# The tanh of the first layer, chunk by chunk from exponentials and a logarithm

## The chip, the cores and the metric

The kernel runs on one core of a Trainium2 chip. The metric is the device time of one execution in microseconds. The core's engines run side by side, each with its own queue of instructions in program order: TensorE (PE, its weight loads as PEld), VectorE (DVE), ScalarE (ACT), GpSimd (POOL), and SyncE (SP), which issues the transfers.

## The reference, cut to what matters

Eight images of 128 channels by 36 x 36 positions (1296 positions) go through two layers. Layer 0 is a convolutional attention block; the part that the change touches is its last step:

```python
xa = jnp.concatenate([x, a_x], axis=1)
h = jnp.tanh(_conv(xa, w_h, 'VALID') + _bias(b_h))
return _conv(h, w_o, 'VALID') + _bias(b_o)
```

Both convolutions are 1 x 1, so they are matrix products over the channels; the second context's part of the first one is the same for every position and is folded into the bias. Layer 1 is additive attention over the 1296 tokens of an image, followed by a mixture of experts:

```python
t = jnp.tanh(q[:, :, None, :] + k[:, None, :, :])
scores = jnp.einsum('bijd,d->bij', t, w) + bw[0]
attn = jax.nn.softmax(scores, axis=-1)
```

All of it is float32.

## The kernel before, in words

**The main loop.** Nearly all the time goes to the scores of layer 1. The kernel does not form the tanh of every query and key pair. It groups the channels by signs into features, so that a score becomes a sum of fractions: a numerator `n` and a denominator `d`, both products of key features and query features on TensorE (line 963; 968 for the remainder), with `1/d` made on ScalarE as Exp(-Ln(d)) (lines 986 and 989), the product on VectorE (lines 1006 to 1017), and sums on VectorE (`accd`) and GpSimd (`accp`, lines 1024 to 1035). A unit of work is one image, one chunk of 432 queries (three chunks an image) and one tile of 128 keys (ten, and a remainder of 16 keys that takes the sixth place in the order). A unit has 12 slots, the remainder unit two; an image has 366 slots, the whole kernel 2928. In a slot, the denominators of three slots ahead are issued (`LAG = 3`, two PSUM buffers for `d`), then the numerators of this one, then the products. Slots go by threes: the first has a Ln and an Exp for itself, the next two have a Ln each and one Exp of double length. Such a three is called a round below. At the end of a unit the summed scores go through an Exp (line 1046).

**The work beside it.** Everything else is written as generators that stand in four lanes: query features, attention sums, gating of the image before, and `background`. The background lane of image b makes image b + 1 ready: normalisation, the convolutions (`conv_keys`, `layer0`), the layer norm over tokens (`tokens`) and the key features (`keys`). A generator says at each `yield` what it needs next: a turn of matmuls (`matmuls(rest)`), a turn without matmuls (`step(rest)`), or to be taken on at once in the same turn (`TAKE`); `rest` is a number of slots to wait. Matmul turns come in the slots 2, 5, 8 and 11 of a unit, one in each round, and a pace (`PACE`, counted in columns of matmuls) decides how many turns of background a lane gets there. Turns without matmuls come before the denominators of a slot, and the lanes but the first don't get them in the slots 1, 4, 7 and 10 (`take_turns`, line 1086). Whatever is issued this way stands in each engine's queue where the loop put it; there is no other scheduler.

**Around the change.** `layer0(b)` loops over the three chunks of 432 positions. Each begins with the query convolution (`conv_turns`, four turns of three matmuls, whose results VectorE adds up), goes on with its attention (scores, Exp at line 473, `tot` sums on GpSimd at line 464, Ln and Exp of the sum at 487 and 488), and ends with the 1 x 1 convolution, whose result VectorE adds to the attention's part into `hp`, a tile of 128 x 1296 (`hpre` in the profile, line 508). After the third chunk one Tanh over the whole tile, with the bias `hb`, is issued at line 511. [...]there is a table load before it, and line 512 asks for the set with Exp and Ln back directly after it. Two slots later the output convolution (`po`) reads `hp`, and VectorE adds it to the image (line 519). For image 0 all this runs before the main loop, for images 1 to 7 in the background lane.

Of the kernel before, what the change touches and what calls it, by code (L numbers as in the profile page):

```python
# [11 lines left out]
AF = mybir.ActivationFunctionType  # L12
ALU = mybir.AluOpType
AX = mybir.AxisListType

NB, C, H, W = 8, 128, 36, 36
# [6 lines left out]
RC = H // NCH  # L23
# [49 lines left out]
def kernel(  # L73
# [28 lines left out]
    nc = tc.nc  # L102
# [29 lines left out]
    with ExitStack() as loop, ExitStack() as score:  # L132
# [22 lines left out]
        def big_tile(name):  # L155
            return big.tile([128, NT * 128], F32, tag="big", name=name)

        def chunk_tile(name):
            return chunks.tile([128, CH], F32, tag="chunk", name=name)

        def aux(name):
            return ps_n.tile([128, 512], F32, tag="n", name=name)
# [40 lines left out]
        ones = const.tile([128, 128], F32, tag="ones", name="ones")  # L203
# [32 lines left out]
        hb = const.tile([C, 1], F32, tag="hb", name="hb")  # L236
# [20 lines left out]
        LNEXP = "natural_log_exp_and_others"  # L257
# [16 lines left out]
        TAKE = (False, 0)  # L274

        def step(rest=1):
            return (False, rest)

        def matmuls(rest=0):
            return (True, rest)  # L280
# [3 lines left out]
        def bmm(out, lhsT, rhs, **kw):  # L284
            behind[0] += max(out.free_size(), 128) + 20
            mm(out, lhsT, rhs, **kw)  # L286
# [9 lines left out]
        def conv_turns(taps, rows, y0, dst, inner):  # L296

            r0, nr = rows
            even, odd = ((1, slice(1, WV, 2)), (0, slice(0, WV, 2))) if inner else (
                (0, slice(0, W, 2)), (0, slice(1, W, 2)))  # L300
            for j in range(4):
                ps = aux("pc")[:, : nr * HW]
                for dy in range(3):
                    bmm(ps, taps[:, dy, j, :],
                        xwin[:, j, (y0 + dy + r0) * HW : (y0 + dy + r0 + nr) * HW],
                        start=(dy == 0), stop=(dy == 2))
                yield TAKE
                ps = ps.rearrange("p (a b) -> p a b", b=HW)
                for (t0, cols), used in ((even, j < 3), (odd, j > 0)):
                    if used:  # L310
                        d = dst[:, :, cols]
                        m = ps[:, :, t0 : t0 + d.shape[-1]]
                        if j == 0 or (j == 1 and cols is odd[1]):
                            nc.vector.tensor_copy(d, m)
                        elif j == 2 and cols is odd[1]:
                            nc.vector.tensor_sub(d, d, m)
                        else:
                            nc.vector.tensor_add(d, m, d)
                yield matmuls()
# [13 lines left out]
        def load_taps(name):  # L333
            if name in raw_taps:
                return raw_taps.pop(name)[0]
            t = big_tile(name)[:, : 12 * C]
            nc.sync.dma_start(t, turned_taps[name])
            return t.rearrange("p (y j c) -> p y j c", y=3, j=4)
# [68 lines left out]
        def grid(t, width):  # L407
            return t.rearrange("p (a b) -> p a b", b=width)

        def conv_keys(b):  # L410
# [3 lines left out]
            for r0, nr in KROWS:  # L414
                yield from conv_turns(
                    taps["k"], (r0, nr), 1, grid(k[:, r0 * WV : (r0 + nr) * WV], WV), True
                )

        def layer0(b):

            r = xs[b][:, :N]
            k = convolved.pop("k")
            while gates:
                yield step()
            wv_t = load_taps("wv_t")
            v = big_tile("v0")
            wq_t = load_taps("wq_t")
            yield matmuls(3)
            for r0, nr in KROWS:
                yield from conv_turns(  # L430
                    wv_t, (r0, nr), 1, grid(v[:, r0 * WV : (r0 + nr) * WV], WV), True
                )
            yield matmuls(1)

            vw = big_tile("vw")[:DT, : NDT * C].rearrange("p (j c) -> p j c", c=C)
            for g in range(0, NDT, 4):
                some = DTILES[g : g + 4]
                tp = aux("pvw")
                for j, (o, n) in enumerate(some):
                    bmm(tp[:n, j * C : (j + 1) * C], v[:, o : o + n], wh_s[:, 1, :],  # L440
                       start=True, stop=True)
                yield TAKE
                full = sum(n == DT for _, n in some)
                nc.vector.tensor_copy(
                    vw[:, g : g + full, :],
                    tp[:DT, : full * C].rearrange("p (j c) -> p j c", c=C),
                )
                for j in range(full, len(some)):
                    n = some[j][1]
                    nc.vector.tensor_copy(vw[:n, g + j, :], tp[:n, j * C : (j + 1) * C])  # L450
                yield matmuls()
            hp = big_tile("hpre")[:, :N]
            for c in range(NCH):
                cols = slice(c * CH, (c + 1) * CH)
                q = chunk_tile("q0")
                yield from conv_turns(wq_t, (c * RC, RC), 0, grid(q, W), False)
                yield matmuls(1)
                tot = chunk_tile("tot0")
                ex = []

                def total(j):
                    n = DTILES[j][1]
                    of = ex[0] if j == 1 else tot
                    nc.gpsimd.tensor_add(tot[:n], of[:n], ex[j][:n])  # L464

                ax = chunk_tile("ax0")
                for j0 in range(0, NDT + 2, 2):
                    for o, n in DTILES[j0 : j0 + 2]:
                        ps = aux("s0")
                        bmm(ps[:n, :CH], k[:, o : o + n], q, start=True, stop=True)  # L470
                        yield TAKE
                        e = chunk_tile("e0")
                        nc.scalar.activation(e[:n], ps[:n, :CH], AF.Exp)  # L473
                        ex.append(e)
                        if len(ex) > 2:
                            total(len(ex) - 2)
                        yield matmuls()
                    if j0 == 0:
                        continue
                    if j0 == NDT:  # L480
                        total(NDT - 1)
                        yield matmuls(3)
                        ri = chunk_tile("ri0")
                        pt = aux("pt0")
                        bmm(pt[:, :CH], ones[:DT], tot[:DT], start=True, stop=True)
                        yield TAKE
                        nc.scalar.activation(ri, pt[:, :CH], AF.Ln)
                        nc.scalar.activation(ri, ri, AF.Exp, scale=-1.0)
                        yield matmuls()

                    pa = aux("pa0")[:, :CH]
                    for j in (j0 - 2, j0 - 1):
                        n = DTILES[j][1]
                        bmm(pa, vw[:n, j, :], ex[j][:n], start=(j == j0 - 2), stop=(j == j0 - 1))
                    yield TAKE
                    if j0 == 2:
                        nc.vector.tensor_copy(ax, pa)
                    elif j0 < NDT:
                        nc.vector.tensor_add(ax, pa, ax)
                    else:  # L500
                        nc.vector.tensor_add(pa, pa, ax)
                        nc.vector.tensor_mul(ax, pa, ri)
                    yield matmuls()
                px = aux("px1")
                bmm(px[:, :CH].rearrange("p (a b) -> p a b", b=W), wh_s[:, 0, :],
                   xpad[:, 1 + c * RC : 1 + (c + 1) * RC, 1 : 1 + W], start=True, stop=True)
                yield TAKE
                nc.vector.tensor_add(hp[:, cols], px[:, :CH], ax)
                yield matmuls()
            yield step(2)  # L510
            nc.scalar.activation(hp, hp, AF.Tanh, bias=hb)
            nc.scalar.preload_act_table_set(LNEXP)
            yield matmuls(2)
            for c in range(NCH):
                cols = slice(c * CH, (c + 1) * CH)
                po = aux("po0")
                bmm(po[:, :CH], wo_s, hp[:, cols], start=True, stop=True)
                yield TAKE
                nc.vector.scalar_tensor_tensor(
                    r[:, cols], po[:, :CH], bo_s, r[:, cols], ALU.add, ALU.add  # L520
                )
                yield matmuls()
# [611 lines left out]
        for p, (u, k) in enumerate(slots):  # L1134
            b, c, j = units[u]
# [172 lines left out]
    for h in range(NB // 2):  # L1308
        for c in range(NCH):
            cols = slice(c * CH, (c + 1) * CH)  # L1310
# [71 lines left out]
```

## Time and profile before

| what | value |
|---|---|
| median of three runs | 6135.24 us (6124.2 to 6139.08) |
| profiled execution, its own time | 6138.18 us |
| its span, first to last instruction | 6136.4 us |
| mean granted TensorE clock | 0.982 |
| Tanh (line 511), eight of 128 x 1296 | 1.376 us each |
| table loads (lines 511 and 512), eight each | 1.283 us each |
| accp addition on GpSimd (line 1026) | 2.023 us each |

The profile shows one execution. A busy share is an average over the span, and a matmul's end is modelled, so a busy TensorE is not one at its peak. A row of a group gives the line, engine, operation, tiles, shapes and count, then the busy us, the mean ns of one, and how long the engine sat idle before them. In an answer in order of time, the first number is the start in us, the second the length, and a bracket gives the idle time before it and what ended it. The granted clock is the share of full speed that the throttle left to TensorE.

### The profile page before, as it was taken

To read this page: it belongs to the slowest core of one execution; us is meant where nothing else is said; L and a number is where in the kernel's file an instruction comes from. 1 tells how busy PE (TensorE), PEld (TensorE's weight loads), DVE (VectorE), ACT (ScalarE), POOL (GpSimd) and SP (SyncE) were. 2 spreads that over 40 slices of the span, in tenths; PEclk is the share of its full clock that TensorE was granted. 3 is DMA by queue.
4 is the path that set the end of the run, shared out by engine and by line. 5 is a ranking of instruction groups with operands and counts; after the bars stand their busy time and mean duration, and the time that the engine had idled before them with its cause. 6 is when DMAs were issued, how large, how long until landed. Compare 5 with 4: busy or idle time off the path is not lost.

```text
span 6136.4 us, 94187 instructions
## 1 busy us (share of the span) xinstructions
PE 5669.6 (92%) x33480; PEld 2924.0 (48%) x33480; DVE 4787.2 (78%) x9521; ACT 5331.3 (87%) x5851; POOL 4595.9 (75%) x2819
## 2 busy tenths in 40 slices
PE   7999999999999999999999999999999999988886
PEld 5554455544554445544445444454455544534433
DVE  4787878878788788877788777887878878788882
ACT  1999898998989989889998999899998998999990
POOL 4777777787778867778687777877777777777870
PEclk9999999999999999999999999999999999999997
DMA  1200021001110011100111001110011001110008
GB/s 44 73 34 22 25 75 39 20 25 33 67 38 20 26 47 52 37 24 26 59 37 42 22 20 65 40 37 22 25 67 47 21 25 33 57 49 26 28 20 297
DMA packets 151528, 270.95 MB, mean 44 GB/s; under 512 B 45648, under 2 KB 76752, under 8 KB 151056
## 3 DMA queue, kind: packets, MB, share of 16 engines
q1 hardware_dynamic: 151056, 264.92, 13.0%
q8 instruction: 264, 4.33, 0.3%
q14 instruction: 208, 1.70, 0.1%
HBM read 200.41 MB, written 64.19 MB: 43 GB/s over the span
## 4 chain that ended last, share of the span: by engine, by line
PE 54%; DVE 16%; ACT 15%; issue 11%; POOL 2%; DMA 1%; SPq 0%; DVEq 0%; ACTq 0%; POOLq 0%
PE d L963 18%; PE n L963 12%; ACT lq L986 11%; PE pa L286 7%; DVE rp L1017 7%; DVE n L1011 5%; PE pc L286 5%; PE s L286 3%; DVE accd L1013 2%; PE pq L286 2%; PE pk L286 1%; PE d L968 1%; PE n L968 1%; ACT e L1046 1%; DMA w<-in_weight_dram 1%
## 5 line engine op out<-in xcount | busy, mean ns | idle before, releaser
L1026 POOL TENSOR_TENSOR accp<-accp,rp 128x864 f32<-128x864 f32 x1440 | 2912.8, 2023 | 989.4 <-DVE rp L1017 946.2
L963 PE MATMUL d<-qf,kf 32*128 32x432 f32 (+1 forms) x11520 | 2791.6, 563 | 264.8 <-ACT lq L986 259.6
L963 PE MATMUL n<-qf,kf 32*128 32x432 f32 (+1 forms) x11520 | 3001.7, 556 | 28.4 <-DVE rp L1017 10.0
L986 ACT ACTIVATE lq<-d 128x864 f32<-128x864 f32 x2928 | 2481.1, 877 | 471.2 <-PE n L963 288.8
L1017 DVE TENSOR_TENSOR rp<-n,lq 128x432 f32<-128x432 f32 x3912 | 2182.0, 601 | 760.7 <-PE n L963 606.0
L989 ACT ACTIVATE lq<-lq 128x864 f32<-128x864 f32 (+1 forms) x1944 | 2495.9, 1284 | 61.6
L963 PEld LDWEIGHTS d<-qf,kf 32*128 32x128 f32 (+1 forms) x11520 | 1026.4, 185 | 1445.5 <-ACT lq L986 1106.0
L963 PEld LDWEIGHTS n<-qf,kf 32*128 32x128 f32 (+1 forms) x11520 | 1263.3, 186 | 700.1 <-issue 293.8
L1013 DVE TENSOR_TENSOR accd<-n,accd 128x432 f32<-128x432 f32 x1440 | 867.8, 603 | 24.7
L1011 DVE TENSOR_TENSOR n<-n,lq 128x432 f32<-128x432 f32 x1440 | 810.8, 607 | 58.3 <-PE n L963 36.8
L1024 POOL TENSOR_TENSOR accp<-rp 128x864 f32<-128x864 f32 x240 | 485.1, 2021 | 290.3 <-DVE rp L1017 287.7
L286 PE MATMUL pa<-xh,e 128*108 128x129 f32 x1920 | 254.8, 281 | 35.2 <-DVE accd L1013 28.0
L286 PEld LDWEIGHTS pa<-xh,e 128*108 128x108 f32 x1920 | 221.0, 174 | 129.9 <-DVE accd L1013 103.0
L1035 POOL TENSOR_TENSOR accd<-accp,accd 128x432 f32<-128x432 f32 x240 | 266.1, 1109 | 18.8
L1033 POOL TENSOR_TENSOR accp<-accp 128x432 f32<-128x432 f32 x240 | 264.7, 1103 | 11.9
L713 POOL TENSOR_SCALAR qf<-qf,cs_s 128x432 f32<-128x432 f32 x192 | 260.0, 1364 | 9.3 <-ACT qf L712 9.3
L464 POOL TENSOR_TENSOR tot<-tot,e 116x432 f32<-116x432 f32 x192 | 212.2, 1105 | 9.0 <-ACT e L473 4.6
L286 PE MATMUL s<-q,k 128*116 128x432 f32 x480 | 207.0, 547 | 8.1 <-DVE accd L1013 5.6
L473 ACT ACTIVATE e<-s 116x432 f32<-116x432 f32 x240 | 116.1, 520 | 99.3 <-PE s L286 98.1
L286 PE MATMUL pa<-e,vw 116*128 116x432 f32 x480 | 196.8, 532 | 0.5
L286 PEld LDWEIGHTS pk<-xT,a_k 128*128 128x128 f32 x1408 | 164.9, 193 | 54.2 <-DVE accd L1013 43.5
L1006 DVE TENSOR_TENSOR accd<-n,lq 128x432 f32<-128x432 f32 x240 | 144.1, 600 | 50.1 <-PE n L963 29.7
(213 smaller groups left out, 3796.2 us busy)
## 6 DMA issues: line engine op xcount, KB each, us to landing
kf<-kd SPq DMA_DIRECT2D x239, 512.0 KB
kd<-ks SPq DMA_DIRECT2D x158, 256.0 KB
w<-in_weight_dram SPq DMA_DIRECT2D x32, 1024.0 KB
wk_t<-wk_t_d SPq DMA_DIRECT2D x7, 768.0 KB
wv_t<-wv_t_d SPq DMA_DIRECT2D x7, 768.0 KB
wq_t<-wq_t_d SPq DMA_DIRECT2D x7, 768.0 KB
x<-in_x_dram SPq DMA_DIRECT2D x8, 648.0 KB
t<-tokd SPq DMA_DIRECT2D x96, 54.0 KB
```

What stands on the lines that cost most here:

```text
L286: mm(out, lhsT, rhs, **kw)
L713: nc.gpsimd.tensor_scalar(qf[:, 1, :], qf[:, 0, :], cs_s[:, q : q + 1], None, ALU.mult)
L963: mm(outs[h][:, :CH], kf[rows[h], q, :], qf_of[b, c, q][rows[h], part, :], start=True, stop=True)
L986: nc.scalar.activation(lq[:, o : o + n, :], d[:, :n, :CH], AF.Ln)
L989: nc.scalar.activation(some, some, AF.Exp, scale=-1.0)
L1011: mult(ns[h], ns[h], lq[:, o + h, :])
L1013: nc.vector.tensor_add(live["d"], ns[h], live["d"])
L1017: mult(rp[:, h, :], n, lq[:, o + h, :])
L1024: nc.gpsimd.tensor_add(live["p"], live["r"], rp)
L1026: nc.gpsimd.tensor_add(live["p"], live["p"], rp)
L1033: nc.gpsimd.tensor_add(s[:, 0, :], s[:, 0, :], s[:, 1, :])
L1035: nc.gpsimd.tensor_add(d, s[:, 0, :], d)
```

## The change

For images 1 to 7 the Tanh over the whole tile and its two table loads go. In their place, tanh(y) = 1 - 2 / (1 + exp(2y)) is computed for each chunk of 432 columns, in place in `hp`, in four steps: add the bias and limit to 15 (GpSimd); Exp of twice the value (ScalarE); Ln of it plus 1 (ScalarE); Exp of minus that, followed by times -2 plus 1 (ScalarE, then GpSimd). Exp and Ln are in the set of tables that the main loop uses. The steps of the first and second chunk are taken up one by one, after each of the four `TAKE`s of the next chunk's query convolution; where two of its turns fall into one turn of the loop, two steps are issued together. The steps of the third chunk are turns without matmuls, one slot apart, and `po` follows two slots after the last one. By the order of instructions `po`, the token transposes and the key features of each of these images come three slots (one round) later than before. Image 0 keeps the Tanh. In the changed kernel's text lines after 418 are numbered up to 27 higher.

```diff
+        def tanh_parts(h):
+
+            def limited():
+                nc.gpsimd.tensor_scalar(h, h, hb, 15.0, ALU.add, ALU.min)
+
+            def exp():
+                nc.scalar.activation(h, h, AF.Exp, scale=2.0)
+
+            def log():
+                nc.scalar.activation(h, h, AF.Ln, bias=ones[:, 0:1])
+
+            def share():
+                nc.scalar.activation(h, h, AF.Exp, scale=-1.0)
+                nc.gpsimd.tensor_scalar(h, h, -2.0, 1.0, ALU.mult, ALU.add)
+
+            return limited, exp, log, share
+
         def layer0(b):
...
             hp = big_tile("hpre")[:, :N]
+            late = deque()
             for c in range(NCH):
                 cols = slice(c * CH, (c + 1) * CH)
                 q = chunk_tile("q0")
-                yield from conv_turns(wq_t, (c * RC, RC), 0, grid(q, W), False)
+                for says in conv_turns(wq_t, (c * RC, RC), 0, grid(q, W), False):
+                    yield says
+                    if late and says == TAKE:
+                        late.popleft()()
                 yield matmuls(1)
+                assert not late
...
                 nc.vector.tensor_add(hp[:, cols], px[:, :CH], ax)
+                if b > 0:
+                    late.extend(tanh_parts(hp[:, cols]))
                 yield matmuls()
-            yield step(2)
-            nc.scalar.activation(hp, hp, AF.Tanh, bias=hb)
-            nc.scalar.preload_act_table_set(LNEXP)
+            if b == 0:
+                nc.scalar.activation(hp, hp, AF.Tanh, bias=hb)
+                nc.scalar.preload_act_table_set(LNEXP)
+            while late:
+                yield step(1)
+                late.popleft()()
             yield matmuls(2)
```

## The prediction

> **What bounds the kernel now.** I read the page's busy table first, then the groups of the operations touched, then the windows around one tanh, and last the order of time on ScalarE at the three kinds of place where the change puts its work.
>
> ```profile
> PE 5669.6 (92%) x33480; PEld 2924.0 (48%) x33480; DVE 4787.2 (78%) x9521; ACT 5331.3 (87%) x5851; POOL 4595.9 (75%) x2819
> ```
>
> Three engines are close to full. A round of three pairs (three Ln, one short and one long Exp) never takes under 5.0 us, because ScalarE needs .87 + .92 + 1.65 + 1.64 us for it; rounds that also carry background matmuls are longer and set by TensorE. So neither engine "is" the bound: each added or removed piece must be priced in its own round. The groups for the pieces:
>
> ```profile
> L488 ACT ACTIVATE ri<-ri 128x432 f32<-128x432 f32 x24 | 13.5, 563 | 0.8
> L511 ACT ACTIVATE hpre<-hpre,hb 128x1296 f32<-128x1296 f32 x8 | 11.0, 1376 | 1.2 <-DVE hpre L508 1.1
> L511 ACT ACT_TABLE_LOAD x8 | 10.3, 1283 | 0.1
> L512 ACT ACT_TABLE_LOAD x8 | 10.3, 1283 | 0.1
> L713 POOL TENSOR_SCALAR qf<-qf,cs_s 128x432 f32<-128x432 f32 x192 | 260.0, 1364 | 9.3 <-ACT qf L712 9.3
> ```
>
> One tanh of today is 1.283 + 1.376 + 1.283 = 3.94 us of ScalarE in one piece. What that does to TensorE, in windows around the last image's tanh (columns: stretch, length, busy us of TensorE matmuls, weight loads, VectorE, ScalarE, GpSimd, granted clock, DMA):
>
> ```profile
> 5132.00:5137.40 5.40, 4.82 (x28) 2.25 (x24) 5.21 (x10) 5.32 (x7) 4.14 (x3) 1.00 0.00 0
> 5137.40:5142.30 4.90, 1.02 (x10) 0.31 (x8) 2.22 (x4) 4.83 (x4) 4.29 (x4) 1.00 0.17 27
> 5142.60:5149.40 6.80, 5.96 (x18) 2.05 (x15) 2.86 (x5) 6.36 (x6) 0.61 (x2) 0.50 0.01 4
> 5149.50:5156.00 6.50, 6.13 (x37) 2.90 (x35) 5.75 (x11) 3.86 (x5) 3.92 (x3) 1.00 0.00 0
> ```
>
> TensorE works 1.02 of 4.90 us while the tanh runs, and then gets half the clock for 6.8 us. The trace's clock record has such a stretch of 6.8 us straight after the tanh of each of images 1 to 7. ScalarE in order of time there:
>
> ```profile
> 5134.77 0.87 ACT L986 ACTIVATE lq<-d 128x864 f32<-128x864 f32 x1
> 5136.51 0.87 ACT L986 ACTIVATE lq<-d 128x864 f32<-128x864 f32 x1
> 5137.40 1.28 ACT L511 ACT_TABLE_LOAD   x1
> 5140.08 1.28 ACT L512 ACT_TABLE_LOAD   x1
> 5141.38 0.89 ACT L986 ACTIVATE lq<-d 128x864 f32<-128x864 f32 x1
> 5143.85 0.87 ACT L986 ACTIVATE lq<-d 128x864 f32<-128x864 f32 x1
> 5152.08 0.89 ACT L986 ACTIVATE lq<-d 128x864 f32<-128x864 f32 x1 [2.88 <-PE n L963]
> ```
>
> The rounds starting at 5134.77 and 5143.85 take 9.1 and 8.2 us, where undisturbed ones take 5.0 to 6.
>
> [...]L1046, with one, takes 0.640 us against 0.563 for L488. [...]no row of the trace has a two-operation tensor_scalar on GpSimd.
>
> **The parts.** Removed, seven times: two loads and the long Tanh, 7 x 3.94 = 27.6 us of ScalarE. Added, 21 times: an Exp (0.56, by L488), a Ln with a pointer bias (0.60, between L488 and L1046) and an Exp (0.56) = 1.73, so 36.3 us of ScalarE, and 42 tensor_scalar on GpSimd. Those I take at the 1.36 of L713; from below 1.10 (the tensor_tensor of that shape, L1033); from above 2.4, if the second operation costs as much per column as the first (0.610 us at 128 columns, L377, and 1.364 at 432 give 2.48 ns a column and 0.29 fixed). 42 x 1.36 = 57 us on an engine idle a quarter of the time. Taken as sums: ScalarE +8.7 us. But place decides:
>
> (a) Third chunk, where the tanh was. The order of instructions says: clamp on GpSimd, Exp after the Ln that ends at 5137.38, Ln one long Exp later, last Exp within the next round; the output matmuls `po` come one round later than before. The accp addition ahead of the clamp ends at 5136.24, the clamp at 5137.6, so ScalarE waits 0.25 us; then 0.56. First round: 2.66 + 0.25 + 0.56 + 0.89 + 1.64 + 0.60 = 6.6 us instead of 9.1. Second: .87 + .92 + .87 + .56 + .89 + 1.64 = 5.7 instead of 8.2, now at the full clock and without `po`. That is 5.0 us; `po` (1.6 us of TensorE) lengthens a later round by about 0.8 (the round from 5152.08, with 1.7 us of transposes, takes 5.5; such rounds run from 5.5 to 6.1). Saved: 4.2 us an image, 29.4 in all. Without the clock's recovery it would be about 2.
>
> (b) First chunk of images 2 to 7. Clamp a whole round ahead of the Exp; Exp and Ln are put together before a Ln that waits for the remainder's matmuls (idle 1.31 us), the last Exp where 1.41 us are idle. 1.17 and 0.56 us fit: nothing. If TensorE stopped being late there it would be 1.7 us an image.
>
> (c) Second chunk of images 2 to 7, and first chunk of image 1. Here the convolution issues two of its turns in one turn of the loop, so clamp and Exp are issued together, and the clamp stands behind that round's accp addition. Image 2, ScalarE then GpSimd:
>
> ```profile
> 1322.90 1.64 ACT L989 ACTIVATE lq<-lq 128x1728 f32<-128x1728 f32 x1
> 1326.02 0.89 ACT L986 ACTIVATE lq<-d 128x864 f32<-128x864 f32 x1 [1.47 <-PE n L963]
> 1331.54 0.87 ACT L986 ACTIVATE lq<-d 128x864 f32<-128x864 f32 x1
> ```
>
> ```profile
> 1324.35 2.02 POOL L1026 TENSOR_TENSOR accp<-accp,rp 128x864 f32<-128x864 f32 x1 [1.18 <-DVE rp L1017]
> 1327.40 2.03 POOL L1026 TENSOR_TENSOR accp<-accp,rp 128x864 f32<-128x864 f32 x1 [1.03 <-DVE rp L1017]
> ```
>
> ScalarE reaches the Exp at 1324.54; the clamp runs from 1326.4 to 1327.8; the Exp ends at 1328.35. The Ln queued behind it, which starts at 1326.02 today, starts 2.3 us later. Behind that Ln wait the next denominators' matmuls (two PSUM buffers, both full), so TensorE stands still as long; from 1326.02 to 1331.54 ScalarE has no gap, and nothing catches up. 7 x 2.3 = 16 us. Then the Ln and last Exp of the six second chunks fall into rounds of 5.0 us without a gap: 6 x 1.1 = 7. [...] A half-clock stretch here slows rounds nearly filled by d, n and convolution, worth some 2.5 us, and hides the 1.1. I take 0.65 x 2.5 = 1.6 each, 11 in all.
>
> (d) Second chunk of image 1: Exp and Ln before a gap of 1.21 us, last Exp in a full round: 0.5 us.
>
> (e) Moved: `po`, the token transposes, the key features and their stores stand one round later. SP issues the same stores and loads; one key load now stands behind two stores. A load is issued two units, some 45 us, ahead of its use: nothing; without that lead the wait for ScalarE's key features (a few us) would show. The normalisation's transposes now stand just ahead of the remainder. They already meet a half-clock stretch in every image, 27 to 38 us after the tanh's, and their rounds last 8.8 to 9.4 us; this may win or lose 1.5 us an image. I put zero. Image 0 keeps its tanh.
>
> Sum: -29.4 + 16 + 7 + 11 + 0.5 = +5 on the profiled execution's 6138.2 (span 6136.4 and 1.8 outside it), 6143. The median shown, 6135.24, is 2.9 lower; I predict 6141.
>
> **Rivals.** First: the wait for the clamp is absorbed. VectorE or GpSimd may run ahead of what a still trace shows, and (c) then costs its 7 us only: 6138 - 29.4 + 7.5, 6116 (6113 against the median). For it: GpSimd idles about 1 us before each addition. Against: the clamp comes behind an addition that itself waits for VectorE.
> Second, on the other side: GpSimd's clamp is slower than L713. At 2.4 us the stop in (c) is 3.3 instead of 2.3, (a) waits one us more, and every stop then loses the clock: (7 + 7) x 1.0 + 7 x 0.9 = 20 more, 6161 against the median. It decides from about 2.0 us. For it: two operations, never seen here. [...]
> Third: the change does nothing that shows, since half-clock stretches come anyway (each image has three or four) and the one removed is replaced in kind: saving of (a) 2 instead of 4.2, 6150 to 6156.
>
> **Numbers.** Near cancellation 0.53, own range 6128 to 6153; the absorbed wait 0.17, around 6113; the slow clamp or lost clock 0.30, 6150 to 6166. A change within 0.3%, about 18 us, can't be told from none here: 6117 to 6154. Range 6116 to 6164, leaving one in ten on either side. Faster 0.17, same 0.53, slower 0.30.
>
> **What would show it.** One tanh with two loads left in the middle of the kernel's start, none later. No half-clock stretch at the third chunk. New waits of ScalarE for GpSimd's hpre, seven near 3.3 us (2.3 beyond the idle of today) and seven near 0.25. Clamp rows near 1.36 us. Half-clock stretches new at the second chunks, in four to five of seven. I am wrong if those waits are short, if the clamp takes 2 us, or if the token rounds change by more than 1.5 us.

## The result, and the profile after

| kernel | median (lowest to highest), us | ratio to before, 95% interval |
|---|---|---|
| before | 6133.40 (6123.24 to 6140.10) | |
| after | 6139.17 (6134.28 to 6150.82) | 1.0015 [1.0008, 1.0021] |

By the medians the change makes the kernel slower by 5.8 us, 0.09%; the ratio, which lies near that of the means (they differ by 8.3 us), says 0.15%. That is less than the 0.3% which the forecast called the least that can be told, but the interval leaves out 1, so a small loss is there. The forecast was 6141, near cancellation. The profiled execution of after is its longest, 6150.82 us with a span of 6149.1, 11.6 over its median; that of before, 6138.18, lies 4.8 over its own.

The busy line of after, to be held against that of before:

```profile
PE 5680.3 (92%) x33480; PEld 2928.4 (48%) x33480; DVE 4784.5 (78%) x9521; ACT 5336.7 (87%) x5893; POOL 4646.1 (76%) x2861
```

ScalarE has 5.4 us more work (forecast 8.7) and GpSimd 50 (forecast 57). Neither is the story. The new instructions, one row per form of the tile `hpre` (columns: line, engine, operation, out<-in, count, ns shortest/median/longest, first and last start in us, shape):

```profile
L422 POOL TENSOR_SCALAR hpre<-hpre,hb x21: 1736/1742/1747, 508.3 to 5150.8; 128x432 f32<-128x432 f32 x21
L425 ACT ACTIVATE hpre<-hpre x21: 546/563/565, 510.0 to 5152.6; 128x432 f32<-128x432 f32 x21
L428 ACT ACTIVATE hpre<-hpre,ones x21: 638/640/657, 516.0 to 5155.5; 128x432 f32<-128x432 f32 x21
L431 ACT ACTIVATE hpre<-hpre x21: 546/547/554, 522.8 to 5158.5; 128x432 f32<-128x432 f32 x21
L432 POOL TENSOR_SCALAR hpre<-hpre x21: 541/553/564, 525.7 to 5159.2; 128x432 f32<-128x432 f32 x21
```

The three ScalarE rows add up to 1.75 us a chunk, as forecast (1.73). The two GpSimd rows differ by three times, although they have the same shape and two operations each: the limit (L422) takes 1.742 us, not 1.364, and the closing multiply and add (L432) 0.553. The waits of after hold one row on the limit (columns: total us, times, longest):

```profile
ACT hpre L425 <- POOL hpre L422: 30.9, 14, 3.7
```

The times of the single instructions split it into seven of some 3.7 us and seven of some 0.7. One of the long ones, at the second chunk of image 2, ScalarE and then GpSimd in order of time (start, length, instruction, in brackets the idle time before it and what ended it):

```profile
1329.29 1.65 ACT L1016 ACTIVATE lq<-lq 128x1728 f32<-128x1728 f32 x1
1334.62 0.56 ACT L425 ACTIVATE hpre<-hpre 128x432 f32<-128x432 f32 x1 [3.69 <-POOL hpre L422]
1335.09 0.87 ACT L1013 ACTIVATE lq<-d 128x864 f32<-128x864 f32 x1
```

```profile
1330.73 2.02 POOL L1053 TENSOR_TENSOR accp<-accp,rp 128x864 f32<-128x864 f32 x1 [1.18 <-DVE rp L1044]
1332.85 1.74 POOL L422 TENSOR_SCALAR hpre<-hpre,hb 128x432 f32<-128x432 f32 x1
1334.67 2.02 POOL L1053 TENSOR_TENSOR accp<-accp,rp 128x864 f32<-128x864 f32 x1
```

ScalarE is free at 1330.94, when the addition ahead of the limit has just begun; it stands through the rest of it and the whole limit. The same stretch in windows (columns: stretch, length, busy us with counts of TensorE matmuls, weight loads, VectorE, ScalarE, GpSimd, granted clock, DMA):

```profile
1325.00:1333.40 8.40, 8.24 (x52) 4.62 (x47) 7.27 (x15) 5.12 (x5) 5.36 (x4) 1.00 0.00 0
1333.40:1337.00 3.60, 0.98 (x6) 0.65 (x8) 2.39 (x5) 2.35 (x4) 3.21 (x2) 1.00 0.00 0
1337.00:1340.50 3.50, 3.50 (x12) 1.89 (x8) 1.12 (x2) 3.47 (x4) 0.83 (x1) 0.51 0.00 0
```

TensorE falls to 0.98 us of work in 3.60, as it did for the Tanh of before (1.02 in 4.90), and then has half the clock (0.51 granted over 3.5 us), for 3.4 us. The third chunk of the last image, ScalarE, where the Tanh was:

```profile
5150.94 0.88 ACT L1013 ACTIVATE lq<-d 128x864 f32<-128x864 f32 x1
5152.55 0.56 ACT L425 ACTIVATE hpre<-hpre 128x432 f32<-128x432 f32 x1 [0.74 <-POOL hpre L422]
5153.02 0.87 ACT L1013 ACTIVATE lq<-d 128x864 f32<-128x864 f32 x1
5155.48 0.64 ACT L428 ACTIVATE hpre<-hpre,ones 128x432 f32<-128x432 f32 x1
5158.52 0.55 ACT L431 ACTIVATE hpre<-hpre 128x432 f32<-128x432 f32 x1
```

The 3.94 us for which the Tanh and its loads held ScalarE are gone; a wait of 0.7 us is left. Of the sixteen table loads at the Tanhs of before two are left, both at the Tanh of image 0 (1.283 us each); the new Exp and Ln have none. To see what each place is worth, I took the times at which the Lns of the main loop start (line 986 in before, 1013 in after), slot by slot, and differenced the two profiles. Summed over images 1 to 7: the seven places with the long wait +28.2 us, the third chunks up to the round that now holds `po` (slots 279 to 290 of an image) -28.9, the first chunks of images 2 to 7 0.0, the rounds of the token transposes (slots 291 to 311, "token rounds" below) +8.3 (5.9 of them in image 1 alone), the start of the images ("normalisation rounds" below) +1.6. These are 9.2 of the 10.0 us by which the main loop of this one profile is longer.

### The profile page after: what moved, and what is told of

The parts are those of the page before. It is cut to its first block, busy times and chain, and to the rows that moved or that the text cites. A ratio compares the mean times of both kernels' runs of the same rounds, so it can differ in the third digit from the quotient of the medians.

```text
span 6149.1 us, 94252 instructions
## 1 busy us (share of the span) xinstructions
PE 5680.3 (92%) x33480; PEld 2928.4 (48%) x33480; DVE 4784.5 (78%) x9521; ACT 5336.7 (87%) x5893; POOL 4646.1 (76%) x2861
## 4 chain that ended last, share of the span: by engine, by line
PE 54%; DVE 18%; ACT 13%; issue 11%; POOL 3%; DMA 1%; SPq 0%; DVEq 0%; ACTq 0%; POOLq 0%
PE d L990 18%; PE n L990 12%; ACT lq L1013 10%; PE pa L286 7%; DVE rp L1044 7%; DVE n L1038 6%; PE pc L286 5%; PE s L286 3%; DVE accd L1040 3%; PE pq L286 2%; PE pk L286 2%; POOL accp L1053 1%; PE d L995 1%; PE n L995 1%; DMA w<-in_weight_dram 1%
## 5 line engine op out<-in xcount | busy, mean ns | idle before, releaser
L1040 DVE TENSOR_TENSOR accd<-n,accd 128x432 f32<-128x432 f32 x1440 | 865.9, 601 | 24.6
L1038 DVE TENSOR_TENSOR n<-n,lq 128x432 f32<-128x432 f32 x1440 | 809.5, 607 | 56.2 <-PE n L990 36.9
L286 PE MATMUL pk<-xT,a_k 128*128 128x128 f32 (+1 forms) x1408 | 180.8, 281 | 1.2
```

The lines of the kernel that those rows point to most:

```text
L1038: mult(ns[h], ns[h], lq[:, o + h, :])
L1040: nc.vector.tensor_add(live["d"], ns[h], live["d"])
```

## The experiments

The theory (A) was that of the forecast: a saving of some 4 us an image at the third chunk, and about as much lost because ScalarE stands before the limit at seven places. The rivals: (B) the waits are absorbed, and something else holds the gain back: the later place of `po`, the extra work, or a clock that is lost anyway.

**The Tanh left out.** What is the whole thing worth? In images 1 to 7 of before, neither Tanh nor loads; that part of the function is not computed.

```diff
-            nc.scalar.activation(hp, hp, AF.Tanh, bias=hb)
-            nc.scalar.preload_act_table_set(LNEXP)
+            if b == 0:
+                nc.scalar.activation(hp, hp, AF.Tanh, bias=hb)
+                nc.scalar.preload_act_table_set(LNEXP)
```

> The kernel before without the tanh and its two table loads for images 1 to 7, nothing in their place (this leaves out the tanh of these images). It prices what the change removes. Theory A: 7 x (4.0 us of ScalarE + about 2 us of half clock) = 42 us less, 6088 to 6098. If the half clock costs nothing by itself: 7 x 4.0 = 28 us less, 6105.

Measured 6091.46 us, ratio 0.9928 [0.9916, 0.9941], so 40 us by the medians and 44 by the means. In the profile the third chunks are shorter by 6.3 us an image: the 3.94 us of ScalarE, and 2.4 of what followed from them. A removed Tanh isn't replaced in kind by other lost clock: 78 us of the main loop are at half the clock, 137 in before (mean granted clock of the two profiled executions 0.986 and 0.982). Some 40 us is about the most that a replacement of these seven can win, as long as nothing else moves.

**The wait put into before.** The Tanh stays; at the same seven places GpSimd makes one tensor_scalar of the limit's form (plus a column of zeros, limit 15) over the chunk, and ScalarE copies the chunk in place, both issued in the same turn of the loop.

```diff
+                    if says == TAKE and b > 0 and c == (1 if b == 1 else 2):
+                        h = hp[:, (c - 1) * CH : c * CH]
+                        if turn == 0:
+                            nc.gpsimd.tensor_scalar(
+                                h, h, pooled_s[:, E * NB : E * NB + 1], 15.0, ALU.add, ALU.min
+                            )
+                        elif turn == 1:
+                            nc.scalar.activation(h, h, AF.Copy)
+                        turn += 1
```

> The kernel before, tanh and all, with only the suspected wait put in at the seven places: a clamp (of no effect on the values) on GpSimd and a Copy on ScalarE that reads it, issued together in the convolution turn as in the changed kernel, in place in hp. Theory A: each place costs 3 to 4 us (a stop of 2.7 and the Copy's half us where no gap takes it, and sometimes a stretch of half clock), so 20 to 28 us on the kernel before, 6152 to 6160. Theory B (the waits are cover for something else and cost little): under 8 us.

Measured 6174.63 us, ratio 1.0067 [1.0054, 1.0081]: 43 us slower, more than either theory had. The wait is made as in after, seven times and no other:

```profile
ACT hpre L466 <- POOL hpre L462: 25.8, 7, 3.7
```

At the seven places the profile is longer by 26.1 us, as theory A had it: six of them are followed by a half-clock stretch of 3.4 us and cost 3.9 to 4.0 each, the seventh is not and costs 2.7. The wait is not absorbed. The rest is elsewhere: the normalisation rounds +7.2 us and the token rounds +8.1, in which the clock record has more half-clock stretches (191 us of the main loop against 137 in before, mean granted clock 0.977 against 0.982). Why more of them come so long after the stops of 3.7 us, this run doesn't say; it stays open.

**The limit one round earlier.** GpSimd gets the limit right behind VectorE's addition, in the turn before; an empty step holds the three ScalarE steps and `po` where after has them. All work of after is done.

```diff
-                    late.extend(tanh_parts(hp[:, cols]))
+                    limited, *rest = tanh_parts(hp[:, cols])
+                    limited()
+                    late.extend((lambda: None, *rest))
```

> The changed kernel with the clamp issued on GpSimd directly after VectorE's addition into hp; its place in the list of steps is an empty step, so Exp, Ln and last Exp stand where they stood. Only the clamp of the second chunks (and of image 1's first) moves, one round earlier. Theory A (the gain of the third chunk is eaten by ScalarE's wait for the clamp): the seven waits of 3.7 us vanish, 7 x 2.7 to 3.7 us less than the changed kernel, so 19 to 26 us under it: 6114 to 6121, that is 12 to 20 us under the kernel before. Theory B (the waits lie in slack, and it is the later po, tokens and keys, or the sum of added work on ScalarE and GpSimd, that eat the gain): within 5 us of the changed kernel, 6135 to 6145.

Measured 6107.31 us (6106.88 to 6109.28), ratio 0.9962 [0.995, 0.9975]: faster than both kernels. Against before after lost 0.15%, this wins 0.38%. The waits of this kernel have no row any more in which ScalarE waits for the limit; the limit itself waits for VectorE, and nobody stands behind it:

```profile
POOL hpre L422 <- DVE hpre L530: 10.2, 14, 0.8
```

At the second chunk of image 2 (ScalarE, in order of time) the Exp now follows its forerunner with no gap:

```profile
1314.75 1.64 ACT L1018 ACTIVATE lq<-lq 128x1728 f32<-128x1728 f32 x1
1316.30 0.55 ACT L425 ACTIVATE hpre<-hpre 128x432 f32<-128x432 f32 x1
1317.86 0.89 ACT L1015 ACTIVATE lq<-d 128x864 f32<-128x864 f32 x1 [1.02 <-PE n L992]
```

The seven places cost 6.1 us instead of 28.2 (1.0 each at the second chunks, nothing at image 1's first), the third chunks save 37.1 instead of 28.9, 5.3 an image, where the wait of 0.74 goes as well (seven of them make 5 of these 8 us). These two, 22.1 and 8.2, make 30 of the 32.5 us by which the ratios of the two kernels differ (0.0053 of 6133). The wait for the limit is what the change lost.

**No limit at all.** VectorE adds the bias in its addition, and there is no limit of 15: first with the three ScalarE steps moved up by one place, then with an empty step in the place of the limit.

```diff
-                nc.vector.tensor_add(hp[:, cols], px[:, :CH], ax)
+                    nc.vector.scalar_tensor_tensor(
+                        hp[:, cols], px[:, :CH], hb, ax, ALU.add, ALU.add
+                    )
...
-                    late.extend(tanh_parts(hp[:, cols]))
+                    late.extend((lambda: None, *tanh_parts(hp[:, cols])))
```

> The changed kernel without the clamp: VectorE's addition into hp takes the bias as well (one scalar_tensor_tensor instead of a tensor_add), and three steps remain (Exp, Ln, last Exp), so they start at the next convolution turn. The clamp to 15 is left out; the values it guards are of the order of 3. Theory A: nothing on ScalarE waits for GpSimd, and po comes back to its old slot; 24 to 32 us under the changed kernel, 6107 to 6115. Theory B: only GpSimd's 37 us of clamps go, on an engine with slack; if the later po is the cost, then its return gains 8 to 29 us too, so this run alone does not tell A from B, the one beside it does.

> As the run without the clamp, but with an empty first step, so that Exp, Ln, last Exp and po stand exactly where they stand in the changed kernel. It left open why the kernel without the clamp (6115 us) was slower than the one with an early clamp (6107 us), though it does less. If po's place is the reason (back in its old round, right behind the third chunk's steps): 6104 to 6109 here, and the third chunk saves 5 us an image instead of 3.4. If VectorE's addition with the bias (667 ns against 607) or something else of the missing clamp is the reason: about 6115 again. If the early clamp itself still costs: under 6103.

Measured 6115.26 us, ratio 0.9972 [0.9961, 0.9983], without the empty step (the second part of the diff left out), and 6108.51, ratio 0.9964 [0.9951, 0.9976], with it. The second equals the early limit (6107.31), so a limit that nobody waits for costs nothing that shows, although it keeps GpSimd busy for 37 us (21 x 1.742). The first saves only 3.4 us an image at the third chunk, against 5.3: there the steps end a round earlier, and `po` is back in its old round. Steps and `po` differ together here, and the seven runs of the first spread from 6105.91 to 6123.72 us, so this pair only suggests that the later `po` of the change helps. The next kernel moves `po` alone.

**`po` later, in before.** The Tanh stays, `po` comes three slots later in images 1 to 7.

```diff
-            yield matmuls(2)
+            yield matmuls(5 if b > 0 else 2)
```

> The kernel before with one change: for images 1 to 7 the output convolution, and with it the tokens and keys, come one round later (a rest of 5 slots after the tanh instead of 2). Theory A: this move costs little, 0 to +8 us on the kernel before (1.2 us an image was seen between the two profiles, most of it in image 1). Theory B: the move costs most of the gain, +20 to +30 us.

Measured 6127.05 us (6118.51 to 6134.14), ratio 0.9993 [0.9985, 1.0001]. The move loses nothing that shows; the interval reaches from a small gain to none. The weight loads and matmuls of `po` in the profile of before, and then in this one (ns shortest/median/longest):

```profile
L286 PEld LDWEIGHTS po<-hpre,w_o x48: 186/286/337, 131.5 to 5150.2; 128*128 128x128 f32 x48
L286 PE MATMUL po<-hpre,w_o x48: 526/527/1087, 131.5 to 5150.6; 128*128 128x432 f32 x48
```

```profile
L286 PEld LDWEIGHTS po<-hpre,w_o x48: 186/190/190, 129.9 to 5151.3; 128*128 128x128 f32 x48
L286 PE MATMUL po<-hpre,w_o x48: 526/526/630, 129.9 to 5151.6; 128*128 128x432 f32 x48
```

In before 26 of the 48 weight loads took over 0.25 us, 22 of them in images 1 to 7: all 26 fell, 23 of them whole, into the half-clock stretch behind their image's Tanh (granted 0.50, 6.8 us long in images 1 to 7, 3.4 in image 0). Moved, those of images 1 to 7 miss it, and in this profile no load takes over 0.19 us. That is 1.6 us an image (0.9 to 2.5), 11 in all, at the third chunk. The token rounds of this profile gave 4.7 of them back, by a half-clock stretch of 20.5 us in image 4.

**Forms of tensor_scalar.** Why is the limit slow? To the kernel without limit, GpSimd gets one more operation over the chunk, of another form for each chunk of odd and even images (where it multiplies by one or adds nought it changes no value). It is there for the lengths alone.

```diff
+            if n == 0:
+                nc.gpsimd.tensor_scalar(h, h, 15.0, None, ALU.min)
+            elif n == 1:
+                nc.gpsimd.tensor_scalar(h, h, 0.0, 15.0, ALU.add, ALU.min)
+            elif n == 2:
+                nc.gpsimd.tensor_scalar(h, h, 1.0, 0.0, ALU.mult, ALU.add)
+            elif n == 3:
+                nc.gpsimd.tensor_scalar(h, h, ones[:, 0:1], 0.0, ALU.mult, ALU.add)
+            elif n == 4:
+                nc.gpsimd.tensor_scalar(h, h, 0.0, None, ALU.add)
+            else:
+                nc.gpsimd.tensor_scalar(h, h, ones[:, 0:1], None, ALU.mult)
```

> A look at GpSimd's durations: the kernel of the first entry with one more GpSimd operation at the early place, of six forms by chunk and image (one or two operations, immediate or pointer operand, min or multiply). The clamp of the changed kernel took 1742 ns and the last multiply-add with two immediates 553 ns, where a multiply by a pointer (L713) takes 1364. If the pointer operand is what costs, the immediate forms take about 550 ns, single ones too; if min is what costs, min forms take 1.3 us or more and the multiply-add by a pointer about 550 ns. The time itself decides nothing: 6105 to 6115.

The rows of `hpre` in its profile, in the order of the diff's cases 3, 4, 5, 0, 1, 2:

```profile
L427 POOL TENSOR_SCALAR hpre<-hpre,ones x4: 618/628/633, 499.9 to 4908.1; 128x432 f32<-128x432 f32 x4
L429 POOL TENSOR_SCALAR hpre<-hpre x4: 1297/1298/1302, 578.7 to 4980.6; 128x432 f32<-128x432 f32 x4
L431 POOL TENSOR_SCALAR hpre<-hpre,ones x4: 1362/1362/1362, 705.0 to 5108.0; 128x432 f32<-128x432 f32 x4
L421 POOL TENSOR_SCALAR hpre<-hpre x3: 1293/1294/1303, 1238.6 to 4174.3; 128x432 f32<-128x432 f32 x3
L423 POOL TENSOR_SCALAR hpre<-hpre x3: 1661/1662/1662, 1311.0 to 4246.7; 128x432 f32<-128x432 f32 x3
L425 POOL TENSOR_SCALAR hpre<-hpre x3: 551/551/552, 1438.7 to 4374.1; 128x432 f32<-128x432 f32 x3
```

Neither a pointer for the number (0.07 to 0.08 us) nor the second operation as such makes it slow: multiply, then add, has two and is the shortest by far. A single addition, a single multiplication and a single minimum take 1.29 to 1.36, and the second operation of the limit adds some 0.37 to that. (The one execution took 6106.48 us, no more than the kernel that it is built on.)

**A short operation in the limit's place.** With the cost by form known: after, but with times 1 plus 0 where the limit stands, and the bias in VectorE's addition. The wait keeps its place and is shorter; there is no limit of 15.

```diff
-                nc.gpsimd.tensor_scalar(h, h, hb, 15.0, ALU.add, ALU.min)
+                nc.gpsimd.tensor_scalar(h, h, 1.0, 0.0, ALU.mult, ALU.add)
```

> The changed kernel with everything in its place, but GpSimd's clamp of 1742 ns replaced by a multiply-add with two immediates (times 1, plus 0), the form that took 551 ns; VectorE's addition takes the bias, and the limit of 15 is left out. One size is changed, the wait's own length. Theory A: the seven long waits of ScalarE fall from 3.7 to 2.5 us, the seven of the third chunks from 0.65 to nothing, so 7 x 1.2 + 7 x 0.65 = 13 us less than the changed kernel, 6126, and half-clock stretches at the seven places get rarer (up to 3 us more). If a wait of any length costs the same (the clock, not the wait): within 5 us of the changed kernel. If only the removal of the wait counts because ScalarE has slack for 2.5 us: about 6107.

Measured 6122.41 us, ratio 0.9987 [0.998, 0.9993], somewhat better than theory A had. Its waits:

```profile
ACT hpre L425 <- POOL hpre L422: 16.6, 7, 2.4
```

An operation that is 1.19 us shorter makes the long waits shorter by 1.3, and the short ones at the third chunk vanish. The seven places now cost 15.9 us instead of 28.2, with no half-clock stretch behind them; that is 2.4 at each second chunk, 1.0 of it for the Ln and the last Exp as before. The third chunks save 31.2, only 2.3 more than in after: 5.0 to 5.6 us in three images, but 3.8 to 4.0 in the four where the half-clock stretch begins a round later, just ahead of `po`. What the addition ahead of the limit's place costs (the wait of 2.4 that is left) is lost in part still.

**Image 0 too.** The kernel without limit and with the empty step, its exponentials for image 0 as well.

```diff
-                if b > 0:
                     late.extend((lambda: None, *tanh_parts(hp[:, cols])))
...
-            if b == 0:
-                nc.scalar.activation(hp, hp, AF.Tanh, bias=hb)
-                nc.scalar.preload_act_table_set(LNEXP)
```

> As the first entry, for image 0 too, which runs before the main loop with nothing beside it: the tanh of 3.94 us with its two loads goes, and the last chunk's Exp, Ln, Exp and multiply-add (0.55 + 0.64 + 0.55 + 0.55 us and their hand-offs) take its place. 0 to 4 us less than the first entry: 6101 to 6108.

Measured 6107.03 us, ratio 0.9962 [0.9949, 0.9974]. In the profile the main loop starts 3 us earlier than in before; but so it does in "`po` later, in before", whose image 0 is unchanged, and the time isn't to be told from 6108.51. So nothing is shown for image 0.

**All of them together.** For each kernel the sum over the two kinds of place, by its one profile, beside its median less that of before in the same comparison, all in us:

| kernel | wait places | third chunks | sum | median less before's | difference |
|---|---|---|---|---|---|
| after | +28.2 | -28.9 | -0.7 | +5.8 | 6.5 |
| Tanh left out | 0 | -44.0 | -44.0 | -40.5 | 3.5 |
| wait put into before | +26.1 | -0.1 | +26.0 | +42.9 | 16.9 |
| limit a round earlier | +6.1 | -37.1 | -31.0 | -24.6 | 6.4 |
| no limit | +3.1 | -24.1 | -21.0 | -16.7 | 4.3 |
| no limit, same places | +6.9 | -36.9 | -30.0 | -23.3 | 6.7 |
| `po` later, in before | 0 | -10.9 | -10.9 | -4.9 | 6.0 |
| short operation | +15.9 | -31.2 | -15.3 | -8.9 | 6.4 |
| no limit, all images | +6.7 | -36.9 | -30.2 | -24.7 | 5.5 |

If these places were all that differs, the last column would be nought; if the profile of before, on which all sums are made, were untypical at just these places, it would be the same everywhere. In eight of nine rows it lies between 3.5 and 6.7. So the two kinds of place account for the differences between these kernels, to 3 us. (By the means, which the ratios follow, the Tanh left out falls out too: two of its five runs are over 10 us faster than the profiled one.) Against before itself, 3.5 to 6.7 us are left. The profiled execution of before lies 4.8 to 6.8 us over its medians in these comparisons; but at the third chunks it agrees to 0.1 us with the wait put into before, which keeps the Tanh, so it doesn't look untypical there. Where they come from stays open. The wait put into before has 10 us more still.

## Why the prediction was right

The mechanism was as forecast: 29 us won at one place and about as much lost at another. That the time and its sign came out as well is in part luck. The two kinds of place sum to -0.7 us in the profile, where the forecast had +5, and the +5.8 between the medians holds 6.5 us from elsewhere, of a kind which nearly every changed kernel shows (last column of the table) and the forecast didn't have. Taken by its parts:

(a) Third chunk: 4.1 us an image (3.2 to 4.8) against 4.2. But it is made up differently. The wait is 0.7 us and not 0.25, mostly because the limit takes 1.74. Of the clock, six of seven third chunks still show a half-clock stretch (of 3.4 us, in image 1 of 6.8), where none was forecast. And 1.6 us come from the move of `po` alone, which leaves the slow stretch ("`po` later, in before"); the forecast had `po` out of the slow round too, but within the return of the full clock, and booked 0.8 for its new place. That these errors cancel is luck.

(b) First chunk of images 2 to 7: nothing, as forecast.

(c) The seven places: 28.2 us, with 0.3 of part (d) in it, against 16 + 7 + 11 = 34. The wait before the Exp is 3.7 us instead of 3.3. The term that was mis-sized is the limit, 1.742 us in the place of the 1.364 of the query features' row: the prediction took another form of tensor_scalar for it. The Ln and the last Exp cost 1.0 at each second chunk against 1.1 (the early limit, and the kernel without one at the same places). The clock was over-priced. The chance of 0.65 and the 2.5 us were both the author's estimate: half-clock stretches came at five of seven, as forecast, but were worth less than the 2.5 us put on each. The two second chunks without one lost 3.7 us each, the four with one 4.1 to 4.2, and image 1's place, which has no Ln and Exp, 3.9. So the stop itself costs 3.7 - 1.0 = 2.7 (forecast 2.3), 19 us in seven, and 2.7 is also what the one place without a stretch cost in the wait put into before; Ln and Exp 6; and the stretches 0.4 to 0.5 in four places and 1.2 in image 1, 3 us where the forecast had 11. With the wait put into before, where no Ln and Exp follow, a stretch cost 1.2 in all six places; that in after it hides part of the Ln and Exp, as the forecast had it, fits this but isn't shown apart.

(d) Second chunk of image 1: 0.3 against 0.5.

(e) The moved `po`, transposes and stores: put at zero, and "`po` later, in before" shows no loss. The token rounds of after's profile, +8.3 us, broke the bound of 1.5 an image, beyond which the forecast called itself wrong, in image 1 (5.9, a half-clock stretch of 20.5 us at 760 us) and in three others by 0.4 (one of them a gain); in the six other kernels that have `po` in the new round and no wait of 3.7 us they change by -1.3 to +4.7 in all. So the move alone doesn't bring the 8.3; what does stays open.

Of the rivals the absorbed wait fell: without the wait the kernel was 32.5 us faster (the early limit), and the wait put into before cost 26 us at its places alone. The slow limit was half right: it is slower than forecast, but 1.74 us lies below the 2.0 from which it was to decide. What stood for it, two operations where the trace of before had one, holds for the limit, whose second operation adds 0.37 us, and not for multiply and add, which take 0.55 us against 1.29 to 1.36 for a single operation. That every longer stop would lose the clock was an estimate too: at 3.7 us two of seven didn't. That the removed stop would be replaced in kind fell with the Tanh left out, which won 40 us, 6.3 an image in place of the 3.94 of ScalarE alone. Two readings of before were off, without weight for the result: from one Tanh to the next its clock record has two to five half-clock stretches, not three or four, and two rounds of the main loop took 4.3 and 4.4 us.

Open: why the changed kernels have 3.5 to 6.7 us more outside these places than before, and the wait put into before 10 on top of that. Half-clock stretches elsewhere differ from kernel to kernel (6.8 us at 756 us in before, 20.5 us at 760 us in after); what decides that was not shown.

## What to carry to other kernels

An operation handed from one engine to another within one turn of a loop made the receiver wait for the giver's queue and the operation itself, here 3.7 us seven times over, 2.7 of them lost each time, though the giver was idle a quarter of the time (GpSimd 76% busy); handed over one turn earlier the same 21 operations cost nothing that shows, and a change that lost 0.15% won 0.38%. Before pricing a new operation by a row of the same shape, see whether that row has the same form: at 128x432 one took 1.36 us, another 0.55. And when a stop is removed, look at what stood in its wake: part of the gain, 1.6 us an image, was matmuls of `po` that had run at half the clock.

## What the runs showed of the hardware

GpSimd's tensor_scalar over 128x432 float32 takes 0.55 us for multiply-then-add with two constants, 0.63 with a pointer for the factor, but 1.29 to 1.36 for a single addition (constant), multiplication (pointer) or minimum (constant), and 1.66 (constants) to 1.74 (pointer) for add-then-minimum. A form with less arithmetic is more than twice as long (1.29 against 0.55 us); I had expected a second operation to cost more or nothing, never to be the cheaper.

After a stop of ScalarE of 3.7 us TensorE had half the clock (0.51 granted in the window shown) for 3.4 us in five places of seven, and the stretch itself cost 0.4 to 0.5 us in four of them and 1.2 in the fifth; put into before, the same stop had such a stretch in six places of seven, at 1.2 us each. With a wait of 2.4 us in the same places no stretch followed.
